# Window attention with a mixture of experts on one core: relative-bias rows as 16 differences per head, computed in two column halves of TensorE

## The chip, the cores and the metric

The kernel runs on one core of a Trainium2 chip. The metric is the time of one execution in microseconds (us) on the device. The engines are called as in the profile: PE (TensorE matmuls), PEld (its weight loads), DVE (VectorE), ACT (ScalarE), POOL (GpSimd) and SP (SyncE, which here issues DMA transfers). All data are float32; in this profile each float32 matmul appears as two MATMUL and two LDWEIGHTS records, two passes over its columns.

## The reference, cut to what matters

The input is x with shape (2, 128, 256, 256). A layer norm over channels is followed by window attention with overlapping keys (queries in 8 x 8 windows, keys in 12 x 12 windows, four heads of 32) and a residual, then by a second layer norm and a mixture of eight experts of which each token takes the best two, again with a residual.

```python
q = q * SCALE
attn = jnp.einsum('bnd,bmd->bnm', q, k)
attn = attn + rel_pos_emb(q, rel_height, rel_width) + FIXED_MASK
attn = jax.nn.softmax(attn, axis=-1)
out = jnp.einsum('bnm,bmd->bnd', attn, v)
...
expert_out = jnp.einsum('bnd,edc->bnec', x, expert_w) + expert_b
gathered = jnp.take_along_axis(expert_out, top_i[..., None], axis=2)
return jnp.einsum('bnk,bnkc->bnc', top_p, gathered)
```

`rel_pos_emb` adds to each score one term that depends on the query and the row distance to the key, and one that depends on the query and the column distance. `FIXED_MASK` leaves only keys at an even row and an even column distance. A query therefore meets 6 x 6 of the 12 x 12 keys, and needs nine relative products for rows and nine for columns, of which it uses six each, at an offset that follows from its place in the window. The softmax of a query does not change if one number is added to all its scores.

## The kernel before

**Planes and strips.** Because of the mask, pixels whose row and column have the same parity only meet one another. The image is worked in 64 strips of 8 rows (32 in each of the 2 images); each strip has 4 planes, one per parity of row and column. A plane has 4 rows of 128 pixels, thus 512 queries, in 32 windows of 4 x 4 queries; its keys are 6 x 10 blocks, each shared by two neighbouring windows. The main loop (line 779) runs over 256 planes n and seven more steps to drain. In step n the kernel does the attention of plane n, projects plane n + 1 ("ahead"), normalizes two double rows (one for the experts, one for a later strip's attention), and works on the experts of rows finished in earlier steps. The experts start at about the seventh step, as they need finished rows.

**Order by hand.** The loop runs under a manual schedule: the order of the instructions on each engine is the order in which the Python generators are advanced with `next`. `scores`, `attend`, `out_project`, `project`, `norms` and `route` are such generators. At the head of each step from n = 6 on, line 793 fills PE's instruction stream with NOPs up to a fixed place in a block of `BLOCK` = 256 instructions, so that the first block limit comes `FIRST_LIMIT` = 95 instructions later.

**Bias.** `wrel` (lines 184 to 196) holds, for each head, nine row and nine column products in a block of 32 columns; together 128 output rows. `project` multiplies it with the plane's 512 queries (`pu`, line 384). DVE transposes `pu` in 32 x 32 blocks to `uT` (line 386), so that queries lie on partitions. `shift` (lines 343 to 355) copies the six products that each query needs, for rows and for columns, into `auT` (line 349) with the offset worked into the access pattern, and transposes back to `au` (line 354), 32 rows per head: six row terms, six column terms, a row of -1e30 for masked places, the rest zero. In `scores`, 16 small matmuls (line 448) multiply `au` with constant 0/1 patterns `keys` and so add the bias to the scores of all keys; line 465 adds the products of queries and keys. ACT takes the exponential (`pT`, line 473).

**The pieces of project**, in order: values(0) (four matmuls to `pvv`, line 369, and ACT's copy to `vv`, line 376); pu and the transpose to uT; `pk` (line 396) with ACT's copies to `kcol` (lines 407 and 414); `pq` (line 418) with ACT's copy to `qs` (line 420); and, later in the step, values(4). All of these, and `plt`, `plg` and `po`, take their PSUM tile in turn from the three buffers of `mm_tile`; a tile can be written when the one that had its buffer three tiles earlier has been read.

**Experts and transfers.** `spread` (line 622) writes gates and normalization factors from `gT` to memory (`gd`, line 633) and reads them back on all partitions: `rb` (line 637), `sb` (line 666) and one `gb` for each expert (line 661, `fetch`). Each fetch is paced by a one-column write of ACT or DVE to its buffer, behind which SP issues the transfer. `times` (line 677) multiplies on DVE or POOL, `product` (line 686) on PE. SP issues all transfers of the loop, in program order.

Of the kernel before, what the change touches and what calls it, by code (L numbers as in the profile page):

```python
# [11 lines left out]
F32 = mybir.dt.float32  # L12
AF = mybir.ActivationFunctionType
ALU = mybir.AluOpType
# [3 lines left out]
P = 128  # L18
HEADS, DH = 4, 32
# [3 lines left out]
NEG = -1e30  # L23
# [16 lines left out]

R = 8
KR, KC = 6, 10
NK = KR * KC
SLOT = 64
BLOCK, FIRST_LIMIT = 256, 95
NU = 9


@with_exitstack
def kernel(
# [31 lines left out]
    work = ctx.enter_context(tc.tile_pool(name="work", bufs=2))  # L84
# [10 lines left out]
    def ctile(shape, name):  # L95
        return const.tile(shape, F32, tag=name, name=name)
# [24 lines left out]
    wall = ctile([P, 4, P], "wall")  # L121
# [51 lines left out]
    relT = []  # L173
    for rname, rsb in zip(("relh", "relw"), relsb):
        pr = mm_tile(f"p_{rname}")
# [5 lines left out]
        relT.append(rT)  # L181
    mid = n_rel // 2
    lo = mid - 2 * (PR - 1)
    relbd = ctile([P, P], "relbd")
    nc.gpsimd.memset(relbd, 0.0)
    for h in range(HEADS):
        hp = slice(h * DH, (h + 1) * DH)
        for j in range(2):
            c0 = h * DH + NU * j
            nc.vector.tensor_copy(  # L190
                relbd[hp, c0 : c0 + NU], relT[j][hp, lo : lo + 2 * NU - 1 : 2]
            )
    wrel = ctile([P, P], "wrel")
    pr = mm_tile("p_wrel")
    nc.tensor.matmul(pr[:, :P], lhsT=wall[:, 0, :], rhs=relbd, start=True, stop=True)
    nc.vector.tensor_copy(wrel, pr[:, :P])

    xn, xcol, kcol = [], [], []
    for i in range(2):
# [8 lines left out]
        nc.gpsimd.memset(kcol[i][:, NP - 1, KC - 1 : NK : KC], 0.0)  # L208


    auT = []
    for i in range(2):
        auT.append(ctile([P, PR, 4, 32], f"auT{i}"))
        nc.gpsimd.memset(auT[i], 0.0)
        nc.gpsimd.memset(auT[i][:, :, :, KR + 6 : KR + 7], NEG)


    def rstd(p4, k0, k1, name):
# [123 lines left out]

    def shift(uT, n, state):

        for j in range(2):
            shifted = uT[:, :, :, NU * j + 3 : NU * j + 9]
            dims = [list(d) for d in shifted.ap]
            dims[1 + j][0] -= 1
            nc.vector.tensor_copy(
                auT[n % 2][:, :, :, 6 * j : 6 * j + 6],  # L350
                bass.AP(shifted.tensor, shifted.offset, dims),
            )
        au = work.tile([P, 2 * NP, PR, 4], F32, tag="au", name=f"au{n}")
        nc.vector.transpose(au.rearrange("p m a s -> p a s m"), auT[n % 2])  # L354
        state["au"] = au

    def project(n, state):

        i, pl = divmod(n, 4)
        xp = xn[i % 2][:, pl // 2, pl % 2]  # L360
        inner = xp[:, 1 : 1 + PR, 1 : PC + 1]
        xl, kk = xcol[pl], kcol[pl]

        vv = work.tile([P, HP, P], F32, tag="vv", name=f"vv{n}")

        def values(t0):
            pv = mm_tile(f"pvv{n}_{t0}")
            for t in range(4):
                nc.tensor.matmul(  # L369
                    pv[:, t * P : (t + 1) * P],  # L370
                    lhsT=xl[:, t0 + t].rearrange("p a k -> p (a k)"),
                    rhs=wv,
                    start=True,
                    stop=True,
                )
# [8 lines left out]
        nc.tensor.matmul(pu, lhsT=wrel, rhs=inner, start=True, stop=True)  # L384
        uT = work.tile([P, PR, 4, 32], F32, tag="uT", name=f"uT{n}", bufs=1)
        nc.vector.transpose(uT, pu.rearrange("p (a m s) -> p a s m", a=PR, s=4))  # L386
        state["shift"] = lambda: shift(uT, n, state)
        yield

        rows = list(ln_rows(i))  # L390
        for part in (rows[-4:], rows[:-4]):
            if not part:
                continue
            pk = mm_tile(f"pk{n}_{part[0]}")
            m = len(part)
            nc.tensor.matmul(  # L396
                pk[:, : m * PC],
                lhsT=wk,
                rhs=xp[:, part[0] : part[0] + m, 1 : PC + 1],
                start=True,  # L400
                stop=True,
            )
# [12 lines left out]
        yield  # L415

        pq = mm_tile(f"pq{n}")
        nc.tensor.matmul(pq, lhsT=wq, rhs=inner, start=True, stop=True)  # L418
# [17 lines left out]
    def scores(n, state):  # L436


        qs, kk, au = state["qs"], state["kk"], state["au"]
        turn = place(n // 4, 0) // 2  # L440
        att = ps_att.tile([P, 4, 512], F32, tag="att", name=f"att{n}")
        sc = att[:, :, 0:HQ]
        for w in range(2):
            for half in range(2):
                rows = slice(half * SLOT, (half + 1) * SLOT)
                for h in range(HEADS):
                    hp = slice(h * DH, (h + 1) * DH)
                    nc.tensor.matmul(
                        sc[rows, h].rearrange("p (t w z) -> p t w z", w=2, z=16)[:, :, w],
                        lhsT=keys[hp, turn, w],  # L450
                        rhs=au[hp, half * NP + w : (half + 1) * NP : 2].rearrange(
                            "p t a s -> p t (a s)"
                        ),
                        start=(w == 0),
                        stop=False,
                    )
        for t in range(HP):
            if t == HP // 2:
                yield
            for half in range(2):  # L460
                rows = slice(half * SLOT, (half + 1) * SLOT)
                m0 = 2 * (half * HP + t)
                for h in range(HEADS):
                    hp = slice(h * DH, (h + 1) * DH)
                    nc.tensor.matmul(  # L465
                        sc[rows, h, 32 * t : 32 * t + 32],
                        lhsT=kk[hp, half * HP + t, :],
                        rhs=qs[hp, m0 : m0 + 2].rearrange("p m a s -> p (m a s)"),
                        start=False,
                        stop=(t == HP - 1),  # L470
                    )
# [257 lines left out]
    n_planes = 4 * len(strips)  # L729
# [43 lines left out]
    gated, ex, nxt = None, NoExperts(), NoExperts()  # L773
# [4 lines left out]
    with tc.manual_schedule(engines={ET.PE, ET.DVE, ET.Activation, ET.Pool, ET.SP}):  # L778
        for n in range(n_planes + 7):
            i, pl = divmod(n, 4)  # L780
            score, attn, outp, ahead, norm, rout = none, none, none, none, none, none
# [84 lines left out]
            gated, nxt = (f, c, made) if made else None, new  # L866
# [59 lines left out]
```

The softmax here doesn't subtract the row's maximum and nothing guards it: scores larger than these inputs give would overflow.

## Time and profile before

| what | value |
|---|---|
| median of 3 runs | 4486.05 us (4485.24 to 4489.12) |
| the profiled execution's own time | 4481.92 us |
| its span, first to last instruction | 4480.1 us |
| mean granted TensorE clock | 0.997 |
| L686 (experts), busy time of PE | 1889.0 us |
| L369 (values), busy time of PE | 594.3 us |
| L384 (pu), busy time of PE | 262.5 us |
| L386 (uT), busy time of DVE | 182.8 us |
| L354 (au), busy time of DVE | 269.2 us |
| L349 (auT), busy time of DVE | 84.4 us |
| DVE waiting for pu before L386 | 77.0 us in 186 waits |

The span is a few microseconds shorter than the execution. A busy time is the union of the instructions' intervals; a matmul's interval overlaps the next one's, so that PE's busy time is not the time that would be saved without them. In a timeline row the numbers are the start, the length, the engine, the line, the operation, the tiles written and read, their sizes and the count; in brackets is the idle time of the engine before it and what ended it. "issue" stands for idle time for which the profile shows no cause.

### The profile page before, as it was taken

The page shows a single profiled execution, that of the slowest core. Times are in us where ns is not written, and L with a number is a line of the kernel's source. Part 1 is how long each engine was busy: PE and PEld are TensorE (multiplying, and loading weights), DVE is VectorE, ACT ScalarE, POOL GpSimd, SP SyncE. Part 2 cuts the span into 40 slices and gives each one's busy share as a digit, 9 for nine tenths or more (in the row PEclk, how much of TensorE's full clock was granted, in tenths as well). Part 3 has the DMA queues.
Part 4 walks back from the last instruction along what each step waited for, and adds up shares of the span by engine and source line. Part 5 has one row for each costly group of instructions (what it writes and reads, how often), then busy time and mean ns, then how long its engine had stood idle before and what let it go on. Part 6 is the DMA issues. An engine that isn't in the chain of part 4 may idle for free. (4 is left out here: it accounts for less than half of the span.)

```text
span 4480.1 us, 224632 instructions
## 1 busy us (share of the span) xinstructions
PE 4422.6 (99%) x96321; PEld 2683.3 (60%) x96321; DVE 3996.2 (89%) x11850; ACT 1467.7 (33%) x4022; POOL 1317.7 (29%) x1815
## 2 busy tenths in 40 slices
PE   7999999999999999999999999999999999999997
PEld 5666666666666666666666666666666666666653
DVE  5899999999899999998989999999999999989887
ACT  3333333333333333333333333333333333333321
POOL 1232323232323233232323232323232323232321
PEclk9999999999999999999999999999999999999999
DMA  2565666566656666666666566666665666566655
GB/s 83 174 191 185 192 185 192 186 191 185 193 184 192 185 191 187 189 188 188 189 187 189 187 190 185 193 183 193 184 193 185 192 185 192 186 191 186 190 164 186
DMA packets 519284, 828.12 MB, mean 185 GB/s; under 512 B 124186, under 2 KB 125850, under 8 KB 518298
## 3 DMA queue, kind: packets, MB, share of 16 engines
q1 hardware_dynamic: 517568, 813.46, 58.3%
q8 instruction: 769, 12.60, 1.1%
q14 instruction: 217, 1.78, 0.2%
q10 hardware_dynamic: 730, 0.29, 0.0%
HBM read 737.95 MB, written 75.56 MB: 182 GB/s over the span
## 5 line engine op out<-in xcount | busy, mean ns | idle before, releaser
L686 PE MATMUL acc<-xe,ew 128*128 128x512 f32 x4096 | 1889.0, 594 | 19.6 <-DVE gb L660 18.8
L686 PEld LDWEIGHTS acc<-xe,ew 128*128 128x128 f32 x4096 | 758.8, 190 | 885.7 <-issue 861.8
L677 DVE TENSOR_TENSOR xe<-xs,gb 128x512 f32<-128x512 f32 x1536 | 950.9, 687 | 10.2 <-PE acc L686 0.7
L681 POOL COPY last<-xe 128x1 f32<-128x1 f32 x256 | 47.9, 187 | 3060.8 <-DVE gb L660 3054.6
L376 ACT COPY vv<-pvv 128x512 f32<-128x512 f32 x512 | 299.8, 586 | 1395.7 <-PE pvv L369 1379.6
L677 POOL TENSOR_TENSOR xe<-xs,gb 128x512 f32<-128x512 f32 x512 | 650.8, 1272 | 5.9 <-PE att L496 2.5
L369 PE MATMUL pvv<-wt,xcol 128*128 128x128 f32 x4096 | 594.3, 288 | 2.5 <-POOL xcol L331 1.5
L369 PEld LDWEIGHTS pvv<-wt,xcol 128*128 128x128 f32 x4096 | 496.4, 191 | 64.8 <-issue 51.8
L272 POOL TENSOR_TENSOR xn<-xt,rb 128x512 f32<-128x512 f32 x249 | 375.0, 1506 | 66.5 <-DMA rb<-gd 55.9
L465 PE MATMUL att<-qs,kcol 32*64 32x32 f32 x32768 | 392.4, 226 | 0.8 <-issue 0.7
L465 PEld LDWEIGHTS att<-qs,kcol 32*64 32x64 f32 x32768 | 391.0, 130 | 1.0 <-issue 1.0
L496 PEld LDWEIGHTS att<-pT,vv 64*32 64x32 f32 x32768 | 348.0, 105 | 39.4 <-issue 2.5
L496 PE MATMUL att<-pT,vv 64*32 64x32 f32 x32768 | 343.2, 200 | 2.3 <-issue 2.3
L473 ACT ACTIVATE pT<-att 128x1024 f32<-128x1024 f32 x256 | 261.9, 1023 | 243.1 <-PE att L465 239.7
L548 ACT ACTIVATE sq<-xt 128x512 f32<-128x512 f32 x505 | 292.7, 631 | 0.0
L354 DVE STREAM_TRANSPOSE au<-auT 128x512 f32<-128x512 f32 x256 | 269.2, 1052 | 9.0
L524 PE MATMUL po<-o,wt 128*128 128x512 f32 x512 | 262.0, 593 | 6.1 <-DVE o L516 3.2
L384 PE MATMUL pu<-xn,wrel 128*128 128x512 f32 x512 | 262.5, 594 | 0.0
L407 ACT COPY kcol<-pk 128x560 f32<-128x560 f32 (+2 forms) x344 | 174.1, 506 | 268.2 <-PE pk L396 265.3
L418 PE MATMUL pq<-xn,wt 128*128 128x512 f32 x512 | 262.0, 593 | 0.0
L396 PE MATMUL pk<-xn,wt 128*128 128x512 f32 (+2 forms) x528 | 261.0, 578 | 0.0
L386 DVE STREAM_TRANSPOSE uT<-pu 128x512 f32<-128x512 f32 x256 | 182.8, 714 | 78.0 <-PE pu L384 77.0
(2697 smaller groups left out, 5243.8 us busy)
## 6 DMA issues: line engine op xcount, KB each, us to landing
gb<-gd SPq DMA_DIRECT2D x2048, 256.0 KB, 4.0
xt<-in_x_dram SPq DMA_DIRECT2D x256, 256.0 KB, 4.9
sb<-gd SPq DMA_DIRECT2D x256, 256.0 KB, 3.5
out_dram<-xt SPq DMA_DIRECT2D x256, 256.0 KB, 4.2
rb<-gd SPq DMA_DIRECT2D x249, 256.0 KB, 3.3
gd<-gT SPq DMA_DIRECT2D x516, 16.0 KB, 3.0
ew<-in_L_ffn_expert_w_dram SPq DMA_DIRECT2D x1, 512.0 KB, 5.0
eb<-in_L_ffn_expert_b_dram SPq DMA_DIRECT2D x1, 512.0 KB, 5.7
```

The costliest lines, as they stand in the source:

```text
L272: eng.tensor_tensor(xn[i % 2][:, :, :, k, 1 : PC + 1], ln1_src(i, k).rearrange("p (y j x) -> p y x j", y=2, x=2), rb.rearrange("p (y j x) ...
L354: nc.vector.transpose(au.rearrange("p m a s -> p a s m"), auT[n % 2])
L369: nc.tensor.matmul(pv[:, t * P : (t + 1) * P], lhsT=xl[:, t0 + t].rearrange("p a k -> p (a k)"), rhs=wv, start=True, stop=True,)
L376: nc.scalar.copy(vv[:, t0 : t0 + 4, :].rearrange("p t c -> p (t c)"), pv)
L384: nc.tensor.matmul(pu, lhsT=wrel, rhs=inner, start=True, stop=True)
L418: nc.tensor.matmul(pq, lhsT=wq, rhs=inner, start=True, stop=True)
L465: nc.tensor.matmul(sc[rows, h, 32 * t : 32 * t + 32], lhsT=kk[hp, half * HP + t, :], rhs=qs[hp, m0 : m0 + 2].rearrange("p m a s -> p (m a ...
L496: nc.tensor.matmul(av[hp, half, 32 * t : 32 * t + 32], lhsT=vv[rows, t, hp], rhs=pT[rows, h, 32 * t : 32 * t + 32], start=True, stop=True,)
L524: nc.tensor.matmul(po, lhsT=wo, rhs=state["o"].rearrange("p f z -> p (f z)"), start=True, stop=True)
L548: nc.scalar.activation(sq, src, AF.Square)
L677: eng.tensor_tensor(self.xe[e], self.xs, self.gb.pop(e), ALU.mult)
L686: nc.tensor.matmul(self.acc, lhsT=ew[:, e, :], rhs=self.xe.pop(e), start=(e == 0), stop=not self.xe)
```

## The change

It has four parts.

1. **Differences.** For each head and direction, `wrel` now holds eight columns: the product weights minus those of the last distance. The ninth would be zero. Since this takes one number per query from all its scores, the softmax is the same. A head has `NB` = 16 columns and all heads together 64.
2. **Two halves.** `pu` is made by two matmuls: the first two rows of queries (256 columns) go to output partitions 0 to 63, the other two to 64 to 127. `uT` has 256 elements per partition for 512. `shift` makes two copies of six row terms on 64 partitions each, two of six column terms on all, and sets with two small memsets the places that read the missing ninth difference. The transpose back (`both`) has 256 elements per partition. Its rows are then 16 per head and half, and a new function `send` moves them with eight transfers, issued by ACT, to `au`, where each head has its 16 rows (of 32) and both halves lie side by side. `au` becomes two constant tiles, one for even and one for odd planes. The bias matmuls of `scores` read it in runs of 8 elements, where they read 16.
3. **Order.** `project` does pu first and values(0) second. In the loop, pu and its shift follow the scores and `spread`, then come values(0), fetch(7) and pk; before, values(0) and fetch(7) stood ahead of `spread`. `send` for plane n + 1 is placed behind the squares of `norms`.
4. **Fetch limit.** `FIRST_LIMIT` is 101 for 95.

```diff
-BLOCK, FIRST_LIMIT = 256, 95
+BLOCK, FIRST_LIMIT = 256, 101
 NU = 9
+NB = 16
...
-            c0 = h * DH + NU * j
-            nc.vector.tensor_copy(
-                relbd[hp, c0 : c0 + NU], relT[j][hp, lo : lo + 2 * NU - 1 : 2]
+            c0 = h * NB + (NU - 1) * j
+            last_d = lo + 2 * (NU - 1)
+            nc.vector.tensor_tensor(
+                relbd[hp, c0 : c0 + NU - 1],
+                relT[j][hp, lo : last_d - 1 : 2],
+                relT[j][hp, last_d : last_d + 1].broadcast_to([DH, NU - 1]),
+                ALU.subtract,
             )
...
-        auT.append(ctile([P, PR, 4, 32], f"auT{i}"))
+        auT.append(ctile([P, 2, 4, 2, NB], f"auT{i}"))
...
+        au.append(ctile([P, 2, 2 * NP, 8], f"au{i}"))
+        nc.gpsimd.memset(au[i], 0.0)
...
     def shift(uT, n, state):
-        for j in range(2):
-            shifted = uT[:, :, :, NU * j + 3 : NU * j + 9]
-            dims = [list(d) for d in shifted.ap]
-            dims[1 + j][0] -= 1
+        to = auT[n % 2]
+        for up, (rows, start) in enumerate(((slice(0, 64), 3), (slice(64, P), 1))):
+            src = uT[rows, :, :, start : start + 6]
...
             nc.vector.tensor_copy(
-                auT[n % 2][:, :, :, 6 * j : 6 * j + 6],
-                bass.AP(shifted.tensor, shifted.offset, dims),
+                to[rows, :, :, :, 0:6].rearrange("p a s h k -> p a (s h) k"),
+                bass.AP(src.tensor, src.offset, dims),
             )
-        au = work.tile([P, 2 * NP, PR, 4], F32, tag="au", name=f"au{n}")
-        nc.vector.transpose(au.rearrange("p m a s -> p a s m"), auT[n % 2])
-        state["au"] = au
...
+        for h in range(2):
+            dims = [list(src.ap[0]), [step, 2], [block - 1, 4], [1, 6]]
+            nc.vector.tensor_copy(
+                to[:, :, :, h, 6:12], bass.AP(src.tensor, src.offset + h * NB, dims)
+            )
+        nc.vector.memset(to[0:64, 0, :, :, 5:6], 0.0)
+        nc.vector.memset(to[:, :, 0, :, 11:12], 0.0)
+        both = work.tile([P, 2 * NP, 8], F32, tag="both", name=f"both{n}")
+        nc.vector.transpose(
+            both.rearrange("p m (a s) -> p a s m", a=2), to.rearrange("p a s h k -> p a s (h k)")
+        )
+        state["both"] = both
+
+    def send(n, state):
+        both = state.pop("both")
+        for up in range(2):
+            for h in range(HEADS):
+                r = (up * HEADS + h) * NB
+                nc.scalar.dma_start(au[n % 2][h * DH : h * DH + NB, up], both[r : r + NB])
...
+        pu = mm_tile(f"pu{n}")
+        for up in range(2):
+            nc.tensor.matmul(
+                pu[up * 64 : (up + 1) * 64, 0 : NQ // 2],
+                lhsT=wrel,
+                rhs=inner[:, 2 * up : 2 * up + 2],
...
+        uT = work.tile([P, 2, 4, 32], F32, tag="uT", name=f"uT{n}", bufs=1)
+        nc.vector.transpose(uT, pu[:, 0 : NQ // 2].rearrange("p (a m s) -> p a s m", a=2, s=4))
+        state["shift"] = lambda: shift(uT, n, state)
+        yield
+
         values(0)
-        yield
-        pu = mm_tile(f"pu{n}")
-        nc.tensor.matmul(pu, lhsT=wrel, rhs=inner, start=True, stop=True)
-        uT = work.tile([P, PR, 4, 32], F32, tag="uT", name=f"uT{n}", bufs=1)
-        nc.vector.transpose(uT, pu.rearrange("p (a m s) -> p a s m", a=PR, s=4))
-        state["shift"] = lambda: shift(uT, n, state)
         yield
...
-                        rhs=au[hp, half * NP + w : (half + 1) * NP : 2].rearrange(
-                            "p t a s -> p t (a s)"
+                        rhs=bias[hp, :, half * NP + w : (half + 1) * NP : 2].rearrange(
+                            "p a t z -> p t a z"
...
     states[0]["shift"]()
+    send(0, states[0])
...
             next(score, None)
-            next(ahead, None)
-            nxt.fetch(7, nc.scalar)
             if gated:
...
                 states[n + 1]["shift"]()
             next(ahead, None)
+            nxt.fetch(7, nc.scalar)
+            next(ahead, None)
             next(ahead, None)
...
             next(norm, None)
+            if n + 1 < n_planes:
+                send(n + 1, states[n + 1])
             next(attn, None)
```

More of the change, by code (lines that the diff above doesn't have):

```diff
@@ L183 @@
     lo = mid - 2 * (PR - 1)
-    relbd = ctile([P, P], "relbd")
+    relbd = ctile([P, HEADS * NB], "relbd")
     nc.gpsimd.memset(relbd, 0.0)
@@ L188 @@
         for j in range(2):
-            c0 = h * DH + NU * j
-            nc.vector.tensor_copy(
-                relbd[hp, c0 : c0 + NU], relT[j][hp, lo : lo + 2 * NU - 1 : 2]
+            c0 = h * NB + (NU - 1) * j
[5 more added lines that the diff above has]
+                ALU.subtract,
             )
-    wrel = ctile([P, P], "wrel")
+    wrel = ctile([P, HEADS * NB], "wrel")
     pr = mm_tile("p_wrel")
-    nc.tensor.matmul(pr[:, :P], lhsT=wall[:, 0, :], rhs=relbd, start=True, stop=True)
-    nc.vector.tensor_copy(wrel, pr[:, :P])
+    nc.tensor.matmul(
+        pr[:, : HEADS * NB], lhsT=wall[:, 0, :], rhs=relbd, start=True, stop=True
+    )
+    nc.vector.tensor_copy(wrel, pr[:, : HEADS * NB])
     xn, xcol, kcol = [], [], []
@@ L208 @@
         nc.gpsimd.memset(kcol[i][:, NP - 1, KC - 1 : NK : KC], 0.0)
-    auT = []
+    auT, au = [], []
     for i in range(2):
-        auT.append(ctile([P, PR, 4, 32], f"auT{i}"))
+        auT.append(ctile([P, 2, 4, 2, NB], f"auT{i}"))
         nc.gpsimd.memset(auT[i], 0.0)
-        nc.gpsimd.memset(auT[i][:, :, :, KR + 6 : KR + 7], NEG)
+        nc.gpsimd.memset(auT[i][:, :, :, :, KR + 6 : KR + 7], NEG)
+        au.append(ctile([P, 2, 2 * NP, 8], f"au{i}"))
+        nc.gpsimd.memset(au[i], 0.0)
     def rstd(p4, k0, k1, name):
@@ L343, in shift @@
     def shift(uT, n, state):
-        for j in range(2):
-            shifted = uT[:, :, :, NU * j + 3 : NU * j + 9]
-            dims = [list(d) for d in shifted.ap]
-            dims[1 + j][0] -= 1
+        to = auT[n % 2]
+        for up, (rows, start) in enumerate(((slice(0, 64), 3), (slice(64, P), 1))):
+            src = uT[rows, :, :, start : start + 6]
+            step, block = src.ap[1][0], src.ap[2][0]
+            dims = [list(src.ap[0]), [step - 1, 2], [block // 2, 8], [1, 6]]
             nc.vector.tensor_copy(
-                auT[n % 2][:, :, :, 6 * j : 6 * j + 6],
-                bass.AP(shifted.tensor, shifted.offset, dims),
-            )
-        au = work.tile([P, 2 * NP, PR, 4], F32, tag="au", name=f"au{n}")
-        nc.vector.transpose(au.rearrange("p m a s -> p a s m"), auT[n % 2])
-        state["au"] = au
+                to[rows, :, :, :, 0:6].rearrange("p a s h k -> p a (s h) k"),
+                bass.AP(src.tensor, src.offset, dims),
+            )
+        src = uT[:, :, :, NU + 2 : NU + 8]
+        step, block = src.ap[1][0], src.ap[2][0]
+        for h in range(2):
[8 more added lines that the diff above has]
+            both.rearrange("p m (a s) -> p a s m", a=2), to.rearrange("p a s h k -> p a s (h k)")
+        )
+        state["both"] = both
[5 more added lines that the diff above has]
+                nc.scalar.dma_start(au[n % 2][h * DH : h * DH + NB, up], both[r : r + NB])
     def project(n, state):
@@ L376, in values @@
             nc.scalar.copy(vv[:, t0 : t0 + 4, :].rearrange("p t c -> p (t c)"), pv)
-        values(0)
-        yield
-        pu = mm_tile(f"pu{n}")
-        nc.tensor.matmul(pu, lhsT=wrel, rhs=inner, start=True, stop=True)
-        uT = work.tile([P, PR, 4, 32], F32, tag="uT", name=f"uT{n}", bufs=1)
-        nc.vector.transpose(uT, pu.rearrange("p (a m s) -> p a s m", a=PR, s=4))
-        state["shift"] = lambda: shift(uT, n, state)
+        pu = mm_tile(f"pu{n}")
+        for up in range(2):
+            nc.tensor.matmul(
+                pu[up * 64 : (up + 1) * 64, 0 : NQ // 2],
+                lhsT=wrel,
+                rhs=inner[:, 2 * up : 2 * up + 2],
+                start=True,
+                stop=True,
+            )
+        uT = work.tile([P, 2, 4, 32], F32, tag="uT", name=f"uT{n}", bufs=1)
+        nc.vector.transpose(uT, pu[:, 0 : NQ // 2].rearrange("p (a m s) -> p a s m", a=2, s=4))
+        state["shift"] = lambda: shift(uT, n, state)
+        yield
+        values(0)
         yield
@@ L436, in scores @@
     def scores(n, state):
-        qs, kk, au = state["qs"], state["kk"], state["au"]
+        qs, kk, bias = state["qs"], state["kk"], au[n % 2]
         turn = place(n // 4, 0) // 2
@@ L448, in scores @@
                     nc.tensor.matmul(
-                        sc[rows, h].rearrange("p (t w z) -> p t w z", w=2, z=16)[:, :, w],
+                        sc[rows, h].rearrange("p (t w a z) -> p t w a z", w=2, a=2, z=8)[:, :, w],
                         lhsT=keys[hp, turn, w],
-                        rhs=au[hp, half * NP + w : (half + 1) * NP : 2].rearrange(
-                            "p t a s -> p t (a s)"
+                        rhs=bias[hp, :, half * NP + w : (half + 1) * NP : 2].rearrange(
+                            "p a t z -> p t a z"
                         ),
```

## The prediction

> **What bounds the kernel now.** I read the page first, then PE's timeline over two planes in the middle, then DVE's, then the waits.
>
> ```profile
> span 4480.1 us, 224632 instructions
> ...
> PE 4422.6 (99%) x96321; PEld 2683.3 (60%) x96321; DVE 3996.2 (89%) x11850; ACT 1467.7 (33%) x4022; POOL 1317.7 (29%) x1815
> ...
> q8 instruction: 769, 12.60, 1.1%
> ```
>
> A busy 99% alone proves little, since matmul ends are modelled. PE's timeline decides: each row is start, length, line; a slot is the distance to the next start.
>
> ```profile
> 2000.49 1.02 PE L686 MATMUL acc<-xe,ew 128*128 128x512 f32 x2
> 2001.45 0.69 PE L448 MATMUL att<-au,keys 32*64 32x128 f32 x32
> 2001.93 1.53 PE L465 MATMUL att<-qs,kcol 32*64 32x32 f32 x128
> 2003.39 1.16 PE L369 MATMUL pvv<-wt,xcol 128*128 128x128 f32 x8
> 2004.39 1.02 PE L384 MATMUL pu<-xn,wrel 128*128 128x512 f32 x2
> 2005.25 1.02 PE L396 MATMUL pk<-xn,wt 128*128 128x512 f32 x2
> 2006.11 1.02 PE L418 MATMUL pq<-xn,wt 128*128 128x512 f32 x2
> ...
> 2012.68 0.40 PE L554 MATMUL plt<-xt,rw 128*32 128x128 f32 x8
> 2012.90 0.40 PE L554 MATMUL plt<-sq,rw 128*32 128x128 f32 x8
> 2013.23 1.16 PE L369 MATMUL pvv<-wt,xcol 128*128 128x128 f32 x8
> ...
> 2016.80 1.02 PE L524 MATMUL po<-o,wt 128*128 128x512 f32 x2
> 2017.66 1.02 PE L686 MATMUL acc<-xe,ew 128*128 128x512 f32 x2
> 2018.61 0.69 PE L448 MATMUL att<-au,keys 32*64 32x128 f32 x32
> ```
>
> No row carries an idle time; a plane takes 2018.61 - 2001.45 = 17.16 us. Some 250 of the 256 planes run so, 4290 of the 4480 us; the first six, without experts, take 11.7 to 12.7 and leave PE idle. So each microsecond off PE's plane counts 250 times, if nothing else steps in. What could is DVE:
>
> ```profile
> 2017.86 0.69 DVE L529 TENSOR_TENSOR xt<-po,xt 128x512 f32<-128x512 f32 x1
> ...
> 2022.09 0.24 DVE L625 STREAM_TRANSPOSE gT<-g 128x64 f32<-128x64 f32 x1
> 2022.61 0.72 DVE L386 STREAM_TRANSPOSE uT<-pu 128x512 f32<-128x512 f32 x1 [0.28 <-PE pu L384]
> 2023.36 0.33 DVE L349 COPY auT<-uT 128x96 f32<-128x96 f32 x2
> 2023.73 1.06 DVE L354 STREAM_TRANSPOSE au<-auT 128x512 f32<-128x512 f32 x1
> ```
>
> L529 starts at 2017.86, 0.04 after po ends (2016.80 + 1.02). From there DVE runs the routing chain, 4.47 us to gT's end, and then waits 0.28 for pu. DVE has no more than about that to spare.
>
> **pu on PE.** Before: slot 2005.25 - 2004.39 = 0.86, two passes of 512 columns. After: two tiles of 128x64, each 2 passes of 256 columns. plt is the nearest row: four tiles side by side do 8 matmuls of 128 columns in 0.22 (2012.90 - 2012.68), while pvv with full width needs 1.00 for 8. Four streams thus cost two passes. If two 64-wide tiles do the same, pu streams 0.43. To this comes a change of tile shape. Drain: acc to L448 takes 0.96 for two passes worth 0.86, so 0.10; plt to pvv takes 0.33 for 0.22, so 0.11. A weight load not hidden: the first pvv group takes 1.00 for 8 x 0.112, so 0.10 for 128 columns, half for 64. Scores to pvv pays one change today; scores to pu to pvv pays two. New slot: 0.43 + 0.05 + 0.10 = 0.58; saving 0.28. Bounds: 0.43 with a free change, 1.01 with both halves one after the other.
>
> The Trainium skill, "TensorEngine Tiling", Key Properties, says that switching the tile shape drains TensorE; it gives no duration and so speaks against the change, and the 0.10 above is that drain. Charging it at both ends of pu would make the slot 0.68, but the one behind the scores is already paid.
>
> **The bias matmuls (L448)** keep 32 instructions and 128 columns; rhs is read in runs of 8 elements instead of 16. No row has runs of 8; at no cost they stay 0.48, at half rate they take 0.43 more. I take none: the full-width rows with runs of 128 (pu) and L448 with 16 stream at the same rate per column.
>
> **DVE.** uT has 256 elements for 512. Transposes take 245 ns at 64, 326 at 128, 714 at 512: 455 at 256. Two copies become four: the old pair takes 0.33; four about 0.50 (two of 96 elements, two of 48). Two dependent memsets, 59 ns each plus a 0.03 step: 0.12. The strided transpose, 1052 at 512, 0.91 to the next start, falls to about 0.48. uT to xs: 2.02 before, about 1.63 after. That ends at xs L671 and later at sT, where DVE then waits for PE: worth nothing by itself.
>
> **Order of buffers, a new wait.** The three mm buffers turn: the fourth tile reuses the first. Before, pq reused pvv(0)'s, which ACT frees early. After, pu is first, so pq reuses pu's and waits for uT. Behind pq on PE stand acc, ones and all of attention. Is uT in time? po end + 0.04 + 4.47 (L529 to gT's end) + 0.03 + 0.455 (uT) + 0.12 (DVE to PE: o ended at 43.44, po's weights came at 43.56) + 0.11 (load) = 5.22 from po's end to pq's start. On PE, pq's start to po's end is 2017.82 - 2006.11 = 11.71. The ring closes in 16.93. PE's own work is 17.16 - 0.28 = 16.88. The ring is longer by 0.05, whatever pu costs, so the plane is **16.93**, saving 0.23. Bounds of uT: 0.36 (half) leaves 16.88; 0.71 (no gain from width) gives 17.19, no saving.
>
> **au by DMA.** Eight issues of 16 KB on ACT's queue, behind sq (L548), which ended at 2009.10 in a stretch where ACT idles 5.25 us until pvv(4). SP's 16 KB issues take 0.52 to 0.61, its gb issues 0.32, ACT's own at the start 0.46 to 1.13. I take 0.45: 3.6 us, done by about 2012.7; behind them wait L114's pacing copy (SP issues that load at 2012.97) and vv at 2014.42. Landing as below, 3.0: au is there by 2015.8, and the scores begin at 2018.3. Hidden; if issue and landing exceed 9 us, the scores wait for the rest.
>
> ```profile
> 2.35 1.13 ACTq L127 DMA_DIRECT2D relw<-in_L_conv_rel_width_dram  x1
> ```
>
> ```profile
> gd<-gT SPq DMA_DIRECT2D x516, 16.0 KB, 3.0
> ```
>
> In the first six planes this cover is short: sq ends at 51.94, the next scores begin at 57.04, au would land at 51.94 + 3.6 + 3.0 = 58.5. With the same for the first plane I add 9 us once (0 to 20).
>
> **The moved steps.** pvv(0) (4 matmuls, ACT's copy) starts 0.58 later; its buffer, plg's, is free at 2002.77. pk starts 0.28 earlier. fetch(7), an ACT copy and a 256 KB transfer, moves on SP behind gd's two writes and rb, which waits for them: from 2005.29 to about 2008.6, landing by 2012.6, while POOL needs it at 2014.93. gd, rb and sb go 0.4 earlier, and nobody waits for them. Cost nothing; beyond 2.3 us more it would stop POOL.
>
> **Fetch blocks.** 769 packets on q8 are three blocks of 256 a plane. 2 x 96321 / 256 = 752 instructions, the rest is filled up. pu adds 4, waits for eight transfers up to 8: it fits in 768. Limits at 95, 351, 607 become 101, 357, 613; the middle one stays at the first acc, behind full-width matmuls. What a bad place costs shows in the unaligned planes:
>
> ```profile
> 33.88 0.38 PE L369 MATMUL pvv<-wt,xcol 128*128 128x128 f32 x1
> 35.28 1.05 PE L369 MATMUL pvv<-wt,xcol 128*128 128x128 f32 x7 [1.02 <-issue]
> ```
>
> I take nothing, upper bound 1.0 a plane.
>
> The Trainium skill, "Runtime: NRT & Kernel Launch", Instruction fetch mechanics, calls the cost of crossing a block mostly hidden; the row above shows 1.02 where it is not, and the measurement decides.
>
> **Sum.** 250 x 0.23 = 58; less 9: 49. Against the profiled execution, 4481.92 (span 4480.1), that is 4433; its median of runs lies 4.1 higher: 4486 - 49, about **4436**.
>
> **Rivals.**
> - *Halves not side by side.* Against it stands plt; for it, that no row has 128x64. If they overlap by half only (0.65 + 0.15 = 0.80), the plane is 17.10: 4486 - 15 + 9 = 4480. If not at all, 1.01, the plane is 17.31: 4486 + 38 + 9 = 4533.
> - *A fetch limit in a dense stretch* (slower). Place: the first limit, among 256 score instructions that pass in 1.46 us, or the middle one. Price 1.0, deciding from 0.23 on: 4486 + 250 x 0.77 + 9 = 4688. Against it: each limit moves by about as much as its code.
> - *ACT issues as slowly as its 1.13.* 8 x 1.13 + 3.0 = 12 us for 9: scores wait 3 us, 4486 + 250 x 2.8, some 5180. It decides from about 0.75 an issue. One row of four is that long, at the start of the program.
> - *Bias rows read at half rate:* 17.31, 4533.
>
> **How the numbers follow.** The forecast 0.72, over a plane of 16.88 to 17.00 and a start of 0 to 20: 4415 to 4465. Something faster still 0.02. Halves partly overlapped 0.05, not at all 0.05; fetch 0.07; slow issues 0.06; bias reads 0.03. The range 4410 to 4485 holds the first three. A measurement here tells 0.2%, 9 us: faster 0.74, same 0.05 (the 4480), slower 0.21.
>
> **What would show it.** Right: L448 to L448 near 16.93; pu's slot near 0.58; uT with no wait, and PE waiting a little at pq for uT; DVE waiting at sT for attention; eight ACTq issues ending before vv. Wrong: idle "issue" time at L465 or L496 (fetch), idle at L448 released by a DMA (au late), a pu slot of 0.8 or 1.0. If PE shows no wait at pq and the plane is 16.88, the ring was counted too long.

## The result and the profile after

The changed kernel takes 4629.13 us (median of 4 runs, 4613.31 to 4630.91) against 4485.65 us (4482.1 to 4489.12): a ratio of 1.0312, interval 1.0288 to 1.0336. It is **slower by 3.1%**; the forecast was 4436. Line numbers below are those of the changed kernel.

The page of the kernel after, its lines on totals, on two DMA queues and on one group of ACT (busy time and mean ns, then the idle time before it):

```profile
span 4626.3 us, 228022 instructions
...
PE 4451.8 (96%) x96833; PEld 2629.9 (57%) x96833; DVE 3802.2 (82%) x12874; ACT 1455.8 (31%) x4022; POOL 1319.9 (29%) x1817
...
q10 hardware_dynamic: 66266, 33.97, 2.8%
q8 instruction: 769, 12.60, 1.1%
...
L118 ACT COPY xt<-onesm 128x1 f32<-128x1 f32 x247 | 47.3, 191 | 1837.7 <-DMA au<-both 1768.0
```

PE, at 99% before, is now at 96%: it waits. The queue q10, which had 730 packets before, carries the eight transfers, and little of DMA's time goes to them. But one group of ACT stands 1768.0 us, 7 us a plane, behind them. L118 is no expensive instruction; it is the first behind the issues.

PE's timeline over one plane (start, length, line, tiles):

```profile
2016.52 1.13 PE L565 MATMUL po<-o,wt 128*128 128x512 f32 x2 [0.20 <-ACT vv L410]
2017.49 1.02 PE L727 MATMUL acc<-xe,ew 128*128 128x512 f32 x2
2018.44 0.69 PE L489 MATMUL att<-au,keys 32*64 32x128 f32 x32
2018.92 1.53 PE L506 MATMUL att<-qs,kcol 32*64 32x32 f32 x128
2020.38 0.65 PE L416 MATMUL pu<-xn,wrel 128*64 128x256 f32 x4
2020.97 1.16 PE L403 MATMUL pvv<-wt,xcol 128*128 128x128 f32 x8
2021.96 1.02 PE L437 MATMUL pk<-xn,wt 128*128 128x512 f32 x2
2022.82 1.02 PE L459 MATMUL pq<-xn,wt 128*128 128x512 f32 x2
2024.10 3.70 PE L727 MATMUL acc<-xe,ew 128*128 128x512 f32 x8 [0.25 <-issue]
```

The slots of the front part are as forecast: scores 0.48 and 1.46, pu 0.59 (2020.97 - 2020.38) for 0.86. Two waits are new: po waits for ACT's second copy to vv, and the first acc comes 1.28 after pq where the slot was 0.86. The two rows of before to compare with, from the planes of the prediction (there pq starts at 2006.11 and po at 2016.80):

```profile
2006.97 3.59 PE L686 MATMUL acc<-xe,ew 128*128 128x512 f32 x8
2014.42 0.59 ACT L376 COPY vv<-pvv 128x512 f32<-128x512 f32 x1 [5.25 <-PE pvv L369]
```

Over 217 planes (12 to 249, without the turn from the first image to the second):

| per plane, us | before | after |
|---|---|---|
| scores to scores, mean | 17.16 (constant) | 17.69 (shortest tenth below 16.94, longest above 18.59) |
| PE's own work (the usual plane before, the shortest after) | 17.16 | 16.89 |
| extra before and within the first acc group | 0 | 0.54 |
| extra between the second acc group and po's end | 0 | 0.22 |

16.89 + 0.54 + 0.22 is 17.65 of the 17.69. Over some 250 planes 0.53 us make 132; with 13.4 us in the first six planes (the seventh scores start at 126.49 for 113.13) that is the 146 us by which the span grew.

What holds ACT shows its timeline in the same plane (ACTq: issues of transfers by ACT):

```profile
2006.75 0.54 ACTq L389 DMA_DIRECT2D au<-both  x1
2006.96 0.63 ACT L589 ACTIVATE sq<-xt 128x512 f32<-128x512 f32 x1
2007.33 1.60 ACTq L389 DMA_DIRECT2D au<-both  x1
2007.49 0.62 ACT L589 ACTIVATE sq<-xt 128x512 f32<-128x512 f32 x1
2008.96 6.79 ACTq L389 DMA_DIRECT2D au<-both  x6
2015.79 0.19 ACT L118 COPY xt<-onesm 128x1 f32<-128x1 f32 x1 [7.68 <-DMA au<-both]
2015.89 0.58 ACT L410 COPY vv<-pvv 128x512 f32<-128x512 f32 x1
2016.37 0.21 ACT L245 ACTIVATE r__112_37968<-u__112_37967 128x8 f32<-128x8 f32 x1
```

The eight issues last from 2006.75 to 2015.75: 9.0 us, where I had written 3.6. Behind them stand L118, which paces SP's next load, the copy to vv that po needs, and the layer norm's L245. Within the 6.79 us there are gaps: the fifth issue starts at 2011.05 and the sixth at 2012.63, while the fourth ended at 2010.21 and the fifth at 2011.57. SP's timeline tells what ACT may have waited for there:

```profile
2006.57 0.33 SPq L678 DMA_DIRECT2D rb<-gd  x1
2006.98 0.38 SPq L702 DMA_DIRECT2D gb<-gd  x1
2007.46 1.47 SPq L707 DMA_DIRECT2D sb<-gd  x1
2009.82 2.14 SPq L702 DMA_DIRECT2D gb<-gd  x3
2016.01 0.33 SPq L119 DMA_DIRECT2D xt<-in_x_dram  x1
```

The transfers of SP and ACT take eight semaphores in turn, in the order of the kernel's list of instructions; before an issue its engine waits until the transfer eight places earlier has landed. By the semaphores in the trace, the fifth issue on ACT waits for gb of fetch(7) (issued at 2006.98), the sixth for sb. And the times agree: in 216 of the 217 planes there is a gap ahead of the fifth issue, and the issue starts 0.02 us after the last update of the semaphore that it shares with that gb; at the sixth it is the same with sb in 206 planes. The Trainium skill, "DMA: Bandwidth & Descriptors", Anatomy of one DMA (a section on GpSimd's path), says that a wait on a semaphore happens on the issuing sequencer and not in the DMA engine. Here it does: ACT stands idle for 0.84 and 1.06 us ahead of these two issues, and the copy to vv, which has nothing to do with the transfers, stands behind them. In the mean of all planes the eight take 8.95 us: 5.39 of issuing (most 0.51 to 0.60, one in six over 0.7 and up to 1.9) and 3.56 of gaps, of them 1.83 ahead of the fifth and 0.98 ahead of the sixth.

The waits as a whole (total us, times, longest), the lines that matter:

```profile
ACT xt L118 <- DMA au<-both: 1768.0, 237, 9.4
...
PEld acc L727 <- issue: 1007.2, 3346, 2.5
...
PEld po L565 <- ACT vv L410: 143.5, 176, 3.0
...
PEld att L489 <- DMA au<-both: 34.1, 43, 3.8
```

The last line is the wait that I had feared, the scores waiting for au. It hardly exists, but the margin is thin: by the semaphores' updates the last of the eight lands 16.87 us after the scores' start in the median, 0.82 ahead of the next scores. In planes of 16.9 us such a landing would be late about every second time. The weight loads of acc idled 861.8 us before, which cost nothing; only the 145 us more speak, and they have no releaser in the profile. The queue of instruction blocks, q8, gives one. Three blocks are fetched a plane. The first of them behind the scores' start now ends 4.27 us after it (median; 3.81 before), and the first acc starts 1.27 to 1.67 us behind that end in nine planes of ten (correlation 0.94 over 216 planes); 73% of the planes wait there.

### The profile page after: what moved, and what is told of

Same layout as the page of the kernel before. It is cut to its first block, busy times and chain, and to the rows that moved or that the text cites. A ratio compares the mean times of both kernels' runs of the same rounds, so it can differ in the third digit from the quotient of the medians.

```text
span 4626.3 us, 228022 instructions
## 1 busy us (share of the span) xinstructions
PE 4451.8 (96%) x96833; PEld 2629.9 (57%) x96833; DVE 3802.2 (82%) x12874; ACT 1455.8 (31%) x4022; POOL 1319.9 (29%) x1817
## 5 line engine op out<-in xcount | busy, mean ns | idle before, releaser
L727 PE MATMUL acc<-xe,ew 128*128 128x512 f32 x4096 | 1912.6, 600 | 95.5 <-issue 76.3
L727 PEld LDWEIGHTS acc<-xe,ew 128*128 128x128 f32 x4096 | 744.1, 191 | 1029.0 <-issue 1007.2
L118 ACT COPY xt<-onesm 128x1 f32<-128x1 f32 x247 | 47.3, 191 | 1837.7 <-DMA au<-both 1768.0
L547 DVE STREAM_TRANSPOSE sT<-att 128x512 f32<-128x512 f32 x256 | 183.5, 717 | 192.4 <-PE att L537 189.8
L565 PE MATMUL po<-o,wt 128*128 128x512 f32 x512 | 272.0, 613 | 41.6 <-ACT vv L410 34.4
L633 ACT ACTIVATE lg<-lg 128x32 f32<-128x32 f32 x256 | 58.7, 229 | 609.5 <-DVE lg L632 609.5
L489 PEld LDWEIGHTS att<-au,keys 32*64 32x64 f32 x8192 | 126.8, 131 | 202.7 <-issue 165.9
```

The lines of the kernel that those rows point to most:

```text
L565: nc.tensor.matmul(po, lhsT=wo, rhs=state["o"].rearrange("p f z -> p (f z)"), start=True, stop=True)
L727: nc.tensor.matmul(self.acc, lhsT=ew[:, e, :], rhs=self.xe.pop(e), start=(e == 0), stop=not self.xe)
```

## The experiments

All times are medians; every ratio is to the kernel before on the same chip. A plane is the mean distance from scores to scores, the hold the time from ACT's first issue for au (in experiment 6, for the spare tile) to the end of its last. Unless said, an edit is made to the changed kernel.

**1. No transfers.** `au` keeps its zeros, so that no relative term and no mask enters the scores; and the limit is 99.

```diff
-BLOCK, FIRST_LIMIT = 256, 101
+BLOCK, FIRST_LIMIT = 256, 99
...
-    send(0, states[0])
...
-            if n + 1 < n_planes:
-                send(n + 1, states[n + 1])
```

> Leaves out the eight transfers of a plane, so the bias rows stay zero and the output lacks the relative bias and the mask; all else is the changed kernel (the limit is 99, since PE has two waits fewer ahead of it). Theory A, ACT held by the eight issues (8.9 us a plane, from 5.7 to 14.7 us after the scores' start), which delays vv, the Ln and Exp, SP's load and, by these, PE's instruction blocks: the plane falls to 16.89 to 16.95, some 4420 us. Theory B, the shorter stretch from the scores to the first acc leaves the instruction block too little time by itself: the first acc still comes up to 1 us late, mean plane 17.3 to 17.4, some 4530 us. If A is the whole and B a small part, the plane is 16.9 to 17.0.

4417.62 us, ratio 0.9844 [0.9829, 0.9858]; the plane is 16.90. PE's timeline:

```profile
2009.13 0.69 PE L489 MATMUL att<-au,keys 32*64 32x128 f32 x32
2009.62 1.53 PE L506 MATMUL att<-qs,kcol 32*64 32x32 f32 x128
2011.07 0.65 PE L416 MATMUL pu<-xn,wrel 128*64 128x256 f32 x4
2011.65 1.16 PE L403 MATMUL pvv<-wt,xcol 128*128 128x128 f32 x8
```

Slots 0.49, 1.45, 0.58: the halves, the runs of 8 elements and the new order bring what was forecast, and the shift chain costs nothing. All of the loss comes with the transfers. (Ahead of acc the trace has four waits of PE fewer than in the changed kernel, not two; experiment 8 comes back to them.)

**2. Half of the transfers**, those of the first two rows; the terms of the other rows and their mask are zero.

```diff
-        for up in range(2):
+        for up in range(1):
```

> Changed kernel with only the four transfers of the first half (the bias rows of the other half stay zero). Theory A as a capacity: ACT may be held from 5.7 to about 12.7 us after the scores' start, when vv is due; eight transfers take 8.95 and end at 14.7, four take about 3.2 (no waits between the first four) and end near 9: plane 16.9, 4420 us. If each transfer cost in proportion, half of the 0.80 us a plane would stay: 17.3, 4520 us.

4424.38 us, 0.9856 [0.9839, 0.9872]; hold 3.20, plane 16.91. Four cost next to nothing, eight cost 0.8 a plane: a capacity, not a price for each.

**3. The block limit eight instructions on.**

```diff
-BLOCK, FIRST_LIMIT = 256, 101
+BLOCK, FIRST_LIMIT = 256, 109
```

> Changed kernel with FIRST_LIMIT 109 for 101: the middle block limit lies four matmul passes (1.7 us) later among the acc matmuls. Theory B: the wait before the first acc (0.54 us a plane) goes, plane about 17.15, 4490 us. Theory A: that wait goes too, but ACT's hold remains and po still waits for vv, and DVE for Ln and Exp; with less slack lost the plane is 17.1 to 17.4, 4490 to 4560 us. No change at 4629 would say that the wait before acc isn't one for an instruction block.

4651.73 us, 1.0374 [1.0358, 1.0389]; hold 9.31, plane 17.86. The wait before acc is gone (the slot is 0.86 again), and po's has grown from 0.22 to 0.89. The waits of this run:

```profile
PEld po L565 <- ACT vv L410: 332.1, 230, 3.6
PE po L565 <- ACT vv L410: 159.0, 160, 2.8
```

So the two waits are not added: acc's delay lay within the time that po would have waited anyway. ACT's hold sets the plane, and a repair at acc alone gains nothing. The run is slower than either theory had it (4560 at most).

**4. The pacing copy ahead of the transfers.** The copy moves ahead on ACT, and the load that it paces moves ahead on SP; L118 and SP's load are then on time.

```diff
+            load_x((n + 9) // 4, (n + 9) % 4, paced=True)
             if n + 1 < n_planes:
                 send(n + 1, states[n + 1])
...
-            load_x((n + 9) // 4, (n + 9) % 4, paced=True)
             new.fetch(3, dve)
```

> Changed kernel with the pacing copy and its load placed ahead of the eight transfers, so that SP's load, fetch(3) and store go out on time, while vv, Ln and Exp still stand behind the transfers. If the road over SP (late 256 KB transfers, late instruction blocks) is what costs: plane 16.9 to 17.2, below 4500 us. If ACT's own road costs (vv and Ln late, po waits): plane 17.5 to 17.8, 4580 to 4660 us, with the wait before acc gone and the wait before po larger, as in the run with limit 109.

4655.0 us, 1.0371 [1.0352, 1.039]; plane 17.76, hold 8.22. L118 starts at 7.5 us after the scores for 14.7, and the extra before acc falls from 0.45 to 0.13, short of the disappearance that I expected; but vv is still copied at 14.4, po waits 0.20 for it (0.22 in the changed kernel, so it did not grow as expected), and now the scores wait for au (0.45 a plane; in the median its last transfer lands 17.9 us after the scores' start). The late loads are thus most of the wait at acc, but not what sets the plane.

**5. The transfers on SP, and on POOL.**

```diff
-                nc.scalar.dma_start(au[n % 2][h * DH : h * DH + NB, up], both[r : r + NB])
+                nc.sync.dma_start(au[n % 2][h * DH : h * DH + NB, up], both[r : r + NB])
```

> The eight transfers issued by SP in place of ACT. Theory A: ACT is free, vv and Ln/Exp are on time, plane 16.9 to 17.1, 4415 to 4470 us; SP's own queue has about 5 us to spare in a plane. Theory C, the transfers themselves or the eight shared semaphores slow whoever issues them: SP's gb, load and store come late by 4 us or more, the plane stays at 17.4 or above, 4550 us or more.

5083.0 us, 1.1333 [1.1316, 1.135]. The plane is 19.62. The 5 us of room that I had counted on SP did not do for a hold of 5.7: its 256 KB transfers go out late and together, and the first acc starts at 7.2 us after the scores, behind a wait that has no releaser in the profile. The same eight issues cost most on SP, which issues all other transfers of the loop.

> The eight transfers issued by POOL, which is busy 29% of the time and idle from about 17.1 - 2.4 us of one plane to 10 us of the next. ACT and SP are as without the transfers. Theory A: 16.9 to 17.1, 4420 to 4470 us, if eight issues take POOL under 8 us. Theory C, the transfers themselves on the DMA engines: 17.4 or more.

With `nc.gpsimd` in the same place: 4520.89 us, 1.0072 [1.0057, 1.0087]; plane 17.27. POOL issues in 0.49 each and without gaps, 4.06 for all; ACT is free. It is 2.3% faster than the change, between the two expectations, and still slower than before: uT on DVE comes later (the weight loads of pq wait 149.6 us for it, 90.9 with ACT issuing), so that 0.17 is lost ahead of pq, and 0.16 more before acc. Why DVE is later was not pursued.

**6. The old kernel with eight idle transfers**, from its `au` into a tile that nobody reads, issued by ACT behind sq.

```diff
+    spare = [ctile([P, 2, 2 * NP, 8], f"spare{i}") for i in range(2)]
...
+                nc.scalar.dma_start(
+                    spare[n % 2][h * DH : h * DH + 16, up].rearrange("p m z -> p (m z)"),
+                    flat[r : r + 16, 0 : NQ // 2],
+                )
```

> Kernel before, plus eight transfers of the same size and at the same place on ACT's queue, into a spare tile that nobody reads. Theory A: slower by what ACT's lateness costs, plane 17.4 to 17.8, 4550 to 4650 us, with ACT held some 9 us. Theory B: nothing, 4486 us, since the limits and the stretch ahead of them are those of before.

4540.2 us, 1.0118 [1.0101, 1.0135]; plane 17.37 for 17.16, hold 6.84. Eight transfers of the same size cost 0.2 here and 0.8 there. Their issues take as long, 5.41; the gaps between them are 1.43 for 3.56. What stands eight places ahead of them differs, which experiment 9 takes up. The result lies between the two theories, and ACT's lateness does not show in it: po and the first acc wait no longer than before. Of the 0.2, 0.18 arise within the 128 matmuls of attention that read vv (L508 of this run's kernel; 1.45 us from the first of them to plt, 1.27 before). No releaser explains them, and the cause stays open; in the changed kernel this stretch takes 1.28.

**7. Two writes to memory and one read back** in place of the eight.

> The bias rows go by three transfers in place of eight: two write the halves to memory (64 KB each), one reads them back to all partitions (256 KB, with filler rows that meet zero keys), all issued by ACT, the read behind the pacing copy. ACT is held about 1.2 us for the writes and until their landing (some 3 us) for the read, to about 10.5 us: plane 16.9 to 17.0, 4420 to 4450 us, faster than both kernels. If the 256 KB read or the wait for the landing pushes vv past 12.7, it is 17.1 or more.

4953.53 us, 1.1029 [1.1005, 1.1053]; plane 18.95. Few issues, but far from the 4420 to 4450 that I expected, since now the way is too long:

```profile
PEld att L501 <- DMA au<-ad: 575.8, 255, 6.4
PE att L501 <- DMA au<-ad: 365.0, 245, 5.6
```

This is how the scores' wait for au looks when it is the limit. Against it, the 34.1 us of the changed kernel are small.

**8. The dose, and dividing the eight.** First six on ACT (the terms of two heads' other rows stay zero), then four or six on ACT and the rest on POOL, with all of the computation.

```diff
+                eng = nc.gpsimd if up else nc.scalar
-                nc.scalar.dma_start(au[n % 2][h * DH : h * DH + NB, up], both[r : r + NB])
+                eng.dma_start(au[n % 2][h * DH : h * DH + NB, up], both[r : r + NB])
```

> Six of the eight transfers, all on ACT; the bias rows of two heads in the second two rows stay zero. Theory (room until 12.7 us): the first four take 3.2 us, and the two more about 0.55 each and the waits that stood ahead of the fifth and sixth in the changed kernel (1.83 and 0.98 us), so that ACT is let go at about 12.5 us: just inside the room, plane 16.9 to 17.1, 4420 to 4480. Rival (each transfer costs its share): three quarters of the way from no_send (4417.6) to the changed kernel (4629.1), 4576; half_send at 4424 already speaks against it.

> Four of the eight transfers stay on ACT (those of the first two rows), the other four go out on POOL at the same place. Nothing is left out. Theory (ACT's hold decides, with room until its copy to vv is due about 12.7 us after the scores' start): ACT's four take about 3.2 us as in half_send and end near 9 us, POOL's four take about 2.0 us (half of the 4.06 of send_pool); the copy to vv and Ln are on time, and the plane falls to 16.9 us, 4420 to 4440 in all, faster than before by 1.0 to 1.5%. Rival A (the number of transfers, or their bytes, in the queues is what costs): still eight per plane, so the plane stays at 17.5 to 17.7, 4580 to 4630. Rival B (each sending engine pays on its own, POOL's share as in send_pool): POOL's experts late by half of what send_pool showed, plane 17.0 to 17.1, 4450 to 4480.

> Six of the eight transfers on ACT, two on POOL, nothing left out. Theory: ACT as in six_send, POOL held 1.0 us: plane 16.9 to 17.1, 4420 to 4480, within 10 us of six_send. Rival A (number of transfers in the queues): 17.5 to 17.7, 4580 to 4630.

Six: 4442.13, 0.9905 [0.9892, 0.9919], hold 6.26, plane 16.97. Four and four: 4455.32, 0.9935 [0.9921, 0.9948], hold 3.00, plane 17.05. Six and two: 4473.32, 0.9977 [0.9968, 0.9987], hold 6.18, plane 17.04. The number of transfers in the queues is not what costs. Two of the times are above what I expected, though: four and four by 15 us, and six and two lies 31 us above six, where I had allowed 10. In four and four a quarter of the planes wait before acc; both lose 0.12 a plane ahead of and within the first acc group.

> Four transfers on ACT and four on POOL, as in split44, and the block limit eight instructions further on (109 for 101). Theory (two costs in the changed kernel: ACT's hold, gone in split44, and the wait for the block of instructions, 0.15 us a plane in split44): the wait before the first acc goes, and nothing takes its place, since the copy to vv starts 12.77 us after the scores, where it is due; plane 16.89 to 16.93, 4418 to 4430. Rival (in split44 what is left is DVE's or POOL's lateness, uT's 0.07 us above all, and not the block): 16.98 to 17.05, 4440 to 4458.

> Four transfers on ACT and four on POOL, limit 101, and the copy that paces the next 256 KB load put ahead of the transfers again, so that it starts at about 7.2 us after the scores for 9.0 in split44. Theory A (the block comes late because the 256 KB loads fall where it is fetched, and they do since the pace copy is late): the wait before acc falls from 0.15 to below 0.05, plane 16.89 to 16.94, 4418 to 4432. Theory B (it comes late through the small transfers' own traffic, or a place at the limit's edge): plane 17.0 to 17.1, 4445 to 4465, as in split44.

> As split44 (four transfers on ACT, four on POOL), with the block limit at 103 for 101. Ahead of the experts' first matmul stand eight instructions more than before the change (four of pu, four waits for the transfers), and the limit was moved by six. Theory (the limit lies one matmul too early, nothing else): with eight the wait before the first acc is gone as with 109, plane 16.93 to 16.98, 4432 to 4444. Rival (109 helped since it is far away, and 103 is as near as 101): 4448 to 4458 as split44.

Four and four with the limit at 109: 4437.99, 0.9897 [0.9882, 0.9912]; plane 16.96, 8 us above the expected range. With the pacing copy first instead: 4461.53, 0.9946 [0.9934, 0.9959], no gain. With the limit at 103: **4437.2**, 0.9895 [0.988, 0.991]. So what is left before acc is the block limit, not the timing of the loads, and two instructions settle it. The trace shows why: PE's sequencer has four waits for semaphores a plane at the scores (none before), and pu four instructions more; the NOPs fall from 14 to 6 a plane. Ahead of acc stand eight instructions more, and the limit had been moved by six. In half_send, with four transfers, the trace has no such waits (and 10 NOPs a plane), so that 101 is late enough there.

**9. fetch(7) back to its old place**, ahead of `spread`; all eight on ACT.

```diff
             next(score, None)
+            nxt.fetch(7, nc.scalar)
             if gated:
...
-            nxt.fetch(7, nc.scalar)
```

> The changed kernel with fetch(7) put back ahead of spread, where it was before the change; all eight transfers on ACT. Theory A (the fifth issue waits for fetch(7)'s 256 KB to land, the sixth for sb): the fifth now waits for rb, which goes out earlier, so that the hold falls from 8.95 to 7.5 to 8.3 us, plane 17.1 to 17.5, 4480 to 4580. Rival B (the waits only pass to rb and sb, which land as late): hold 8.7 to 9.1, 4610 to 4640.

4489.1 us, 1.0007 [0.9998, 1.0017]. The hold falls to 7.31 (the gap ahead of the fifth issue is 1.27 for 1.83, that ahead of the sixth 0.05 for 0.98), po's wait is gone, and the plane is 17.09. In the trace the fifth issue now starts 0.02 us after the landing of rb, in 216 of 217 planes. **One moved 256 KB transfer was worth 140 of the 143 us by which the change was slower than before.** What still waits is acc, 0.19 a plane.

> The changed kernel with two moves and nothing else: fetch(7) ahead of spread as before the change, and the block limit at 103. All eight transfers on ACT. Theory (the place of fetch(7) lengthens ACT's hold, and the limit is one matmul too early): the 0.19 us that fetch7_early still waits before the first acc goes, the hold stays near 7.3, plane 16.90 to 16.98, 4425 to 4450, and so about what was predicted for the change. Rival (the hold of 7.3 then shows as a wait of po for vv, as in limit109): plane 17.1 or more, 4480 or more.

With the limit at 103 as well: 4451.84, 0.9928 [0.9914, 0.9941]; hold 7.44, plane 16.99, at the upper edge of what the theory gave. The timeline of ACT in this kernel:

```profile
2008.28 0.52 ACTq L389 DMA_DIRECT2D au<-both  x1
2008.84 0.61 ACTq L389 DMA_DIRECT2D au<-both  x1
2009.48 6.84 ACTq L389 DMA_DIRECT2D au<-both  x6
2016.37 0.19 ACT L118 COPY xt<-onesm 128x1 f32<-128x1 f32 x1 [6.52 <-DMA au<-both]
2016.46 0.58 ACT L410 COPY vv<-pvv 128x512 f32<-128x512 f32 x1
2017.39 0.21 ACT L245 ACTIVATE r__116_39318<-u__116_39317 128x8 f32<-128x8 f32 x1 [0.35 <-DVE u__116_39317 L244]
```

The hold of this plane, 2008.28 to 2016.32, is 8.0 and one of the longer ones, and yet L245 waits for DVE again, and not for ACT's queue.

> As split44_103 (four transfers on ACT, four on POOL, limit 103), and fetch(7) ahead of spread. With the hold already short at 3.1 us, fetch(7)'s place should be worth little on ACT; what is left in split44_103 (16.96 against 16.89) stands at pk, pq and before the first acc, where DVE's transposes are late behind POOL's issues. Theory: 16.93 to 16.97, 4430 to 4442, the same as split44_103. Rival (fetch(7)'s transfer also collides there): 16.89 to 16.91, 4418 to 4428.

All three repairs: 4440.32, 0.99 [0.9886, 0.9913], the same as without fetch(7)'s; once the hold is 3 us its place is worth nothing.

The holds side by side, from the traces:

| kernel | hold, us | plane, us | po waits, us a plane |
|---|---|---|---|
| split44 | 3.00 | 17.05 | 0 |
| split44_103 | 3.06 | 16.96 | 0 |
| half_send | 3.20 | 16.91 | 0 |
| split62 | 6.18 | 17.04 | 0 |
| six_send | 6.26 | 16.97 | 0 |
| fetch7_early | 7.31 | 17.09 | 0 |
| fetch7_103 | 7.44 | 16.99 | 0.01 |
| pace_first | 8.22 | 17.76 | 0.20 |
| changed kernel | 8.95 | 17.69 | 0.22 |
| limit109 | 9.31 | 17.86 | 0.89 |

The issues start 5.7 us after the scores, and with no hold the copy to vv starts at 12.70: up to 7.0 the hold moves nothing. What po can bear is more, and single planes show it. In the changed kernel, pace_first, limit109, six_send, split62 and the two fetch7 kernels, po waits in no plane with a hold under 8.5 us; above 9.5 it waits 0.53 us in the mean of the changed kernel's planes and 1.45 in limit109's. So ACT's capacity ends between 8.5 and 9 us, and in the changed kernel two planes of three (146 of 217) have a hold above 8.5. The other differences between the planes of the table are mostly waits at acc, and in pace_first also the scores' wait for au.

## Why the prediction was wrong

- **Slots on PE: right.** pu 0.58 as summed (0.583), the bias matmuls at no cost, PE's own plane 16.89 for 16.88.
- **The ring through the three buffers: too long, by little.** uT takes 0.408 for the 0.455 estimated, so the slot from pk to pq stays 0.86; the plane without transfers is 16.90, not 16.93.
- **The shift chain: mis-sized, free.** From uT's start to xs 1.88 for 1.63 (the transposing back takes 0.64 for 0.48). DVE waits at sT as forecast (56.4 us in no_send, 10.6 before).
- **"au by DMA ... Hidden": the step that failed.** "Eight issues of 16 KB ... I take 0.45: 3.6 us" became 8.95, for two reasons. The issue itself takes 0.67 in the mean (5.39 for 8); rows of 0.52 to 0.61 for SP's 16 KB stood beside the 0.45 that I chose. And I counted no waits between them, 3.56. The deciding point was misplaced too: I compared issue and landing with the start of the next scores (9 us), while the copy to vv behind the issues on ACT, which the text names, is ready to start 7.0 us after the first issue, and po waits for it from a hold of 8.5 to 9 on. The landing was mis-sized with it: 14.4 us after the scores' start by the prediction, 16.87 in the median, which is still ahead of the next scores because the plane has grown.
- **The rival "ACT issues as slowly as its 1.13"**, at 0.06, had the right engine and by chance the right length: 8.95 / 8 is 1.12. Its consequence was wrong. au lands in time in most planes, and vv and L118 are late; a plane costs 0.8 more than PE's work and not 2.8 more than before.
- **The moved steps, "Cost nothing": wrong.** I looked at who needs fetch(7)'s data (POOL, 2.3 us of room) and not at who is behind its semaphore. Its transfer had become the one that ACT's fifth issue waits for: 4629.1 to 4489.1 by this line alone (fetch7_early).
- **Fetch blocks, "I take nothing": wrong by a little.** "Each limit moves by about as much as its code" was six for eight. It costs 0.1 a plane with a shorter hold (plane 17.09 to 16.99 in fetch7_103, 17.05 to 16.96 in split44_103). In the changed kernel it is covered by ACT's hold (limit109). The Trainium skill, "Runtime: NRT & Kernel Launch", Instruction fetch mechanics, calls this cost mostly hidden; here it is hidden only where the limit lies right.
- **The first planes:** 13.4 us for the 9 (0 to 20).

With fetch(7) and the limit mended and nothing else, the kernel takes 4451.84, inside the forecast's own range; without any transfers (no_send) it takes 4417.62. What remains open: how much of the longer issues (up to 1.9 us) is due to the traffic, what slows attention in experiment 6, and why the plane of fetch7_103 still varies (one in ten above 17.21). Of the 0.10 a plane that it lies above PE's own work, 0.09 arise within the first acc group, at its first two matmuls and with no releaser in the profile.

## What to carry to other kernels

A transfer's issue is an instruction of its engine: count it with its waits, and compare the end of the last with what that engine owes next, and not only with the moment when the data are needed. Where transfers of several queues share a few semaphores in turn, every moved transfer moves waits of others; list for each issue what stands as many places ahead as there are semaphores. And where one wait covers another, repair the one that sets the period first: the limit at 109 was worth nothing in the changed kernel, and 17 us in the divided one.

## What the hardware showed that I had not expected

- In the changed kernel an issue of 16 KB by ACT takes 0.51 at least; the second to fourth, at a time when SP also issues, 0.8 to 0.9 in the mean and up to 1.9. On POOL each takes 0.49, evenly, and 4.06 for eight.
- Where the block limit lies at acc, TensorE's first matmul there starts some 1.3 us or more after the block's transfer has ended in the trace (1.27, 1.30 and 1.29 at the fifth percentile in the changed kernel, split44 and pace_first). So a block that looks early by a microsecond is late.
- Two 64-column tiles of float32 run side by side: pu takes 0.583 for 0.864, with the change of tile shape; one half after the other would, by an estimate from the same 0.86 for 512 columns, have taken that for the streaming alone.
